# Two attention layers of a four-layer network on one core: the values' bias on VectorE, an earlier flag, and a first normed half block made one stage ahead

## The chip, the cores and the metric

The kernel runs on one core of a Trainium2 chip. The time is the device time of one execution in microseconds. A core has a matrix engine (TensorE, PE in the profile, with its weight loads as PEld), a vector engine (VectorE, DVE), an engine for activation functions (ScalarE, ACT), a general engine (GpSimd, POOL), and queues for transfers (SP is the one used here for weights and outputs). The engines run side by side, each in the order of its own program, and wait for one another by semaphores. Matrix products write to PSUM, a small memory of banks; everything else lies in SBUF, a memory of 128 partitions.

## The reference

The input x is 2 x 512 channels x 32 x 32 positions in float32, so every image is a matrix of 512 x 1024. Four layers follow one another, each on the output of the one before:

- Layer 0: attention on sampled positions with a learned position bias, and then an MLP of two products.
- Layer 1: linear attention with normalized queries and keys.
- Layers 2 and 3: plain attention. The two differ only in the number of groups of the normalization (8 and 32), and the change touches these two. Cut to what is computed:

```
xn   = group_norm(x) * w + b                    # per image
q,k,v = qkv_w @ xn + qkv_b                      # 512 x 1024 each, 8 heads of 64 channels
attn = softmax(q.T @ k * 64**-0.5, axis=keys)   # 1024 x 1024 for each head
out  = v @ attn.T                               # 64 x 1024 for each head
x    = x + proj_w @ out + proj_b
```

Because the weights of a softmax sum to 1, the bias of the values can be added to the result of a head instead of to the values. The kernel does so.

## The kernel before

**Layers and their stages.** `layer0`, `mlp0` and `layer1` end near 2555 us of the span. Layers 2 and 3 are two calls of `attention` (L954), each of two stages. `queries_keys_values` (L990) makes the queries, keys and values of both images; `heads_bounded` (L1205) makes the softmax, the result of the heads, the projection and the sum with x. The x tiles (4 per image, 128 channels x 1024 positions) stay in SBUF from the first layer to the last.

**Normalization.** Means and variances of an image's channels come from `channel_means` (L1168, on VectorE, after an early load of ScalarE's square root table). `group_means` (L1179) averages them over a group by two small TensorE products, and ends with the scale `sc`. `offsets_of_norm` (L1199) makes the offset `off` by two small VectorE instructions. Each is made for image 0 in the stage in front: layer 2's at the end of `layer1` (L907 to L928), layer 3's in the last projections of layer 2's heads (L1301 to L1307). The offsets and the normed tiles come at the beginning of `queries_keys_values`.

**Queries, keys and values.** Each product of 512 x 512 by 512 x 1024 is done by seven products of half size instead of eight (P1 to P7, the order is P1, P2, P3, P6, P7, P5, P4). They need the normed image as four half blocks of 256 channels x 512 positions, and three sums of them. `norm` (L1020) makes half blocks 0, 2, 3, 1 in this order, each by two instructions, c = 0 on VectorE (L1028) and c = 1 on ScalarE (L1026). P1 needs block 0 alone. For each image the products of queries and keys come first (PE, L1046), then those of the values (L1065), with adds on VectorE (L1084) that collect them. The order of the four compute engines in this stage is the order in which the code emits, by a manual schedule (L1089).

**The flag.** The softmax subtracts no maximum as long as the logits are bounded. `largest` (L1149) works out a bound from the squares of queries and keys; it runs after the first three value products of an image. After all value products of image 1, two VectorE instructions make `ok` and `oki` (L1139, L1141), and ScalarE has a small Exp that loads its table ahead (L1143). Every engine reads `oki` into a register, and branches: `heads_bounded` if the bound holds, `heads_general` otherwise (L972). With these inputs the bound holds.

**Heads.** A unit is one image, one pair of heads and one half of the query positions: 2 x 4 x 2 = 16 units, each of 8 steps n, one for each 128 keys. A step is a score product s (L1229, 8 matmuls), an exp from PSUM to an e tile on ScalarE (L1233), an addition of e to one of two running sums, and a value product o (L1258, 8 matmuls, which adds up over the unit in PSUM). The sums: `some` = e0 + e1 + e3 + e5 on POOL (L1238, L1240), `sum` = e2 + e4 + e6 + e7 + some on VectorE (L1243, L1245 twice, L1247). Values follow scores two steps behind. At the end of a unit ScalarE copies one half of o into the place of the queries (L1267) and VectorE adds the other (L1268). `divide` follows at step 4 of the next unit: a product d with ones gives the column sums (L1275), ScalarE copies one half (L1279), VectorE adds the other (L1280), takes the reciprocal (L1281), multiplies (L1283), and ScalarE adds the values' bias (L1284). TensorE's order is written out by hand (L1288 to L1311); that of the other engines is set by the tile scheduler from the dependences.

**Buffers.** The pool `ps_s` has 2 score tiles of two PSUM banks each (tag s), the pool `ps_o` one tile for o and one for d. There are 6 e tiles, one `some`, two `sum`. The pool `norm` lives from layer 1 to the end; the normed half blocks r0 to r6 are in a pool of `queries_keys_values`.

**Projection.** `project_block` (L593) makes 128 rows of the projection of one image by 8 products (L598) and adds bias and x on VectorE (L607). It runs for image 0, then image 1, four blocks each; in layer 3 the output leaves from here by SP. In layer 2 the means of image 0 for layer 3 are taken within: all four `channel_means` and the first product of `group_means` ahead of the second block of image 1, the second product ahead of the third.

**Before layer 1.** Its weights (`layer1_weights`, L776) are loaded by SP, 1.31 MB for the weights and 0.33 MB for a bias spread over all partitions, into a pool whose space layer 0 uses earlier. `lb` tiles of layer 0 (L409) are loaded on the same queue.

Of the kernel before, what the change touches and what calls it, by code (L numbers as in the profile page):

```python
# [11 lines left out]
F32 = mybir.dt.float32  # L12
AF = mybir.ActivationFunctionType
ALU = mybir.AluOpType
# [38 lines left out]
class Net:  # L53
# [730 lines left out]
    def layer1(self, w, bias):  # L784
# [3 lines left out]
        with ExitStack() as ctx:  # L788
# [108 lines left out]
            for b in range(B):  # L897
                for h in range(2):
# [30 lines left out]

# [24 lines left out]
    def attention(self, k: int, weights, out, meanwhile=lambda: None):  # L954
# [3 lines left out]
        with ExitStack() as ctx:  # L958
# [9 lines left out]
            small_logits, got = self.queries_keys_values(k, weights, ones, data, meanwhile)  # L968
            if k == 2:
                self.means_tiles(3, 0)  # L970

            with self.tc.If(small_logits > 0) as cmp:  # L972
                self.heads_bounded(k, ones, data, out)
            with cmp.Else():
                self.heads_general(k, data)
                with ExitStack() as ctx2:
                    proj = self.projection_weights(self.pool(ctx2, f"a{k}_w_p"), k)
                    ps = self.pool(ctx2, f"a{k}_ps_p", 2, psum=True)
                    for b in range(B):
                        for o in range(CT):  # L980
                            acc = ps.tile([P, 2, HF], F32, tag="ps", name=f"pbg{k}{b}{o}")
                            self.project_block(acc, data[b][0], proj, f"pb{k}", b, o, out)
                    if k == 2:
                        for t in range(CT):
                            self.channel_means(3, 0, t)
                        for _ in self.group_means(3, 0, ps.tile([P, 2, HF], F32, tag="ps", name="gm3g")):
                            pass
            return got

    def queries_keys_values(self, k, weights, ones, data, meanwhile):  # L990
# [8 lines left out]
        with ExitStack() as ctx:  # L999
# [20 lines left out]
            def norm(b, r, i, c, eng):  # L1020

                t = 2 * (i // 2) + c
                _, sc, off = self.means[b]
                x = self.xs[b][t][:, (i % 2) * HF : (i % 2 + 1) * HF]
                if eng is act:
                    act.activation(r[i][:, c, :], x, AF.Identity, scale=sc[:, t : t + 1], bias=off[:, t : t + 1])  # L1026
                else:
                    vec.tensor_scalar(r[i][:, c, :], x, sc[:, t : t + 1], off[:, t : t + 1], ALU.mult, ALU.add)  # L1028

            def square(i, t, h, cm):  # L1030

# [56 lines left out]
            engines = {getattr(mybir.EngineType, e) for e in ("PE", "Activation", "DVE", "Pool")}  # L1088
            with self.tc.manual_schedule(engines=engines):  # L1089
                dqk = small.tile([P, CT], F32, tag="dqk", name=f"dqk{k}")  # L1090
                self.offsets_of_norm(k, 0)
                xns = [tiles(0)]
                for i in (0, 2, 3, 1):
                    for c in range(2):
                        norm(0, xns[0], i, c, (vec, act)[c])
                vec.tensor_tensor(dqk, self.colr(f"qb{k}", CT), self.colr(f"kb{k}", CT), ALU.subtract)
                for b in range(B):
                    r = xns[b]
# [26 lines left out]
                    for n, which in enumerate(("P1", "P2", "P3", "P6", "P7", "P5", "P4")):  # L1125
# [4 lines left out]
                        if n == 2:  # L1130
                            while late:
                                late.pop(0)()
                            self.largest(k, b, ones, cm, small, ps_g, flag)
                        if b == 0 and which in ("P1", "P2", "P3", "P7"):
                            i = {"P1": 0, "P2": 2, "P3": 3, "P7": 1}[which]
                            for c in range(2):
                                norm(1, xns[1], i, c, act)
                ok = small.tile([1, B], F32, tag="ok", name=f"ok{k}")
                vec.tensor_scalar(ok, flag, 480.0**2, None, ALU.is_le)  # L1139
                oki = small.tile([1, 1], mybir.dt.int32, tag="oki", name=f"oki{k}")  # L1140
                vec.tensor_tensor(oki, ok[:, 0:1], ok[:, 1:2], ALU.mult)  # L1141
                early = small.tile([P, 1], F32, tag="early", name=f"early{k}")
                act.activation(early, self.cols[:, 0:1], AF.Exp, scale=0.0)  # L1143
# [55 lines left out]
    def offsets_of_norm(self, k, b):  # L1199
# [2 lines left out]
        self.nc.vector.tensor_tensor(off, gm, sc, ALU.mult)  # L1202
        self.nc.vector.tensor_tensor(off, self.colr(f"gn_b{k}", CT), off, ALU.subtract)

    def heads_bounded(self, k, ones, data, out):  # L1205


# [5 lines left out]
        with ExitStack() as ctx:  # L1213
# [56 lines left out]
            def divide(unit):  # L1270
# [10 lines left out]
                nc.vector.reciprocal(t, t)  # L1281
                res = data[b][0][p][:, h * HF : (h + 1) * HF]
                nc.vector.tensor_tensor(res, res, t, ALU.mult)  # L1283
                nc.scalar.activation(res, res, AF.Identity, bias=self.col(f"vb{k}", p))  # L1284

            units = [(b, p, h, {}) for b in range(B) for p in range(CT) for h in range(2)]
            steps = [(unit, n) for unit in units for n in range(NB)]
            with self.tc.manual_schedule(engines={mybir.EngineType.PE}):  # L1288
# [9 lines left out]
                        divide(steps[i - NB][0])  # L1298
                for b in range(B):
                    for o in range(CT):  # L1300
                        if b == 1 and o > 0 and k == 2:  # L1301
                            if o == 1:
                                for t in range(CT):
                                    self.channel_means(3, 0, t)
                                steps = self.group_means(3, 0, ps_o.tile([P, 2, HF], F32, tag="d", name="gm3"))
                            else:
                                next(steps, None)  # L1307
                        acc = ps_s.tile([P, 2, HF], F32, tag="s", name=f"pb{k}{b}{o}")
                        self.project_block(acc, data[b][0], proj, f"pb{k}", b, o, out)
                        if b == o == 0:  # L1310
                            divide(units[-1])  # L1311

    def heads_general(self, k, data):
        with ExitStack() as ctx:
# [214 lines left out]
```

## Time and profile before

| quantity | value |
|---|---|
| median of 3 runs | 3470.4 us (3470.14 to 3472.15) |
| profiled execution: time, span | 3472.31 us, 3470.5 us |
| mean granted clock of TensorE | 0.995 |
| busy: TensorE, VectorE, ScalarE, GpSimd | 3403.5, 2296.9, 2034.2, 2078.3 us |
| layer 2: first product of queries and keys | 2553.39 us |
| layer 2: first score | 2705.72 us |
| layer 3: first product of queries and keys | 3013.08 us |
| layer 3: first score | 3163.97 us |
| one unit of the heads in regular running | 15.25 us |

The profile is of one execution. A line of its timeline gives start, busy time, engine, line of the code, operation, the tile written and the tiles read, their shapes and the count of instructions gathered in the line; in brackets stands how long the engine had been idle, and whose work ended that. The view of waits adds such idle times by the line that waited and the line it waited for. TensorE's matmuls are pipelined and their ends are modelled, so distances between starts say more than ends. A wait of an engine that has time to spare costs nothing.

### The profile page before, as it was taken

The numbers are of one execution on the slowest core, as the hardware profiler recorded it, in microseconds if no ns is written. First come the engines' busy times: TensorE is split into PE (matmuls) and PEld (weight loads), VectorE is DVE, ScalarE is ACT, GpSimd is POOL, SyncE is SP. The second block draws the span as 40 slices with busy tenths as digits, with TensorE's granted clock in tenths as the row PEclk, the third lists the DMA queues.
The fourth block names the chain that finished last, engine by engine and source line by source line (L and its number), as shares of the span: only waits on it lengthen the run. The fifth ranks groups of instructions, "written<-read, shape, count | busy, mean of one in ns | idle before, by whom it ended". The sixth has DMA issues, their size and how long they took to land.

```text
span 3470.5 us, 60111 instructions
## 1 busy us (share of the span) xinstructions
PE 3403.5 (98%) x25280; PEld 1260.8 (36%) x25280; DVE 2296.9 (66%) x2507; ACT 2034.2 (59%) x2132; POOL 2078.3 (60%) x1584
## 2 busy tenths in 40 slices
PE   7999999999999999999999999999999999999999
PEld 2333333333333333333333334444646433454333
DVE  6877777778767567777766665565465566455664
ACT  5877877887887687887887762111111566113661
POOL 4778777777787577787788873442233444234441
PEclk9999999999999999999999999999989999999999
DMA  5878777887887577777788862110000000000001
GB/s 152 157 140 159 150 155 146 157 156 143 158 158 143 111 156 146 155 156 146 152 163 156 162 162 78 37 49 24 1 1 25 25 1 2 1 0 13 1 1 50
DMA packets 103246, 342.64 MB, mean 99 GB/s; under 512 B 12720, under 2 KB 14384, under 8 KB 100144
## 3 DMA queue, kind: packets, MB, share of 16 engines
q0 software_dynamic: 73296, 266.90, 40.7%
q1 hardware_dynamic: 28656, 69.68, 6.7%
q8 instruction: 202, 3.31, 0.4%
q10 hardware_dynamic: 1008, 2.06, 0.2%
q14 instruction: 84, 0.69, 0.1%
HBM read 67.27 MB, written 4.46 MB: 21 GB/s over the span
## 4 chain that ended last, share of the span: by engine, by line
PE 88%; DVE 7%; ACT 2%; POOL 1%; issue 1%; DMA 0%; ACTq 0%; DVEq 0%; SPq 0%; POOLq 0%
PE hp L486 45%; PE s L1229 6%; PE o L1258 6%; DVE h L455 3%; PE pb L598 3%; PE sim L518 3%; PE qk20P L1046 1%; PE qk30P L1046 1%; PE m_0P L649 1%; PE m_5P L649 1%; PE m_3P L649 1%; PE m_2P L649 1%; PE qk31P L1046 1%; PE qk21P L1046 1%; PE m_6P L649 1%; PE m_1P L649 1%
## 5 line engine op out<-in xcount | busy, mean ns | idle before, releaser
L486 PE MATMUL hp<-h,w 128*32 128x512 f32 x16384 | 1833.1, 594 | 5.5 <-DVE h L455 3.5
L455 DVE CUSTOM_DVE_ANT_1 h<-tx,bank 128x1024 f32<-128x1024 f32 x1024 | 1180.9, 1216 | 333.2 <-PE hp L486 310.2
L491 ACT ACTIVATE h<-hp,magb 128x1024 f32<-128x1024 f32 x1024 | 1122.3, 1111 | 418.9 <-PE hp L486 417.0
L486 PEld LDWEIGHTS hp<-h,w 128*32 128x32 f32 x16384 | 545.6, 110 | 1215.5 <-issue 1119.7
L478 POOL DMA_DIRECT2D h<-h x509 | 451.7, 1025 | 393.2 <-ACT h L497 334.2
L504 POOL TENSOR_TENSOR h<-h,h 128x1024 f32<-128x1024 f32 x255 | 613.6, 2406 | 21.3
L502 POOL TENSOR_SCALAR h<-h,flip 128x1024 f32<-128x1024 f32 x256 | 448.3, 1751 | 0.9 <-ACT h L491 0.9
L1233 ACT ACTIVATE e<-s 128x1024 f32<-128x1024 f32 x256 | 254.7, 1020 | 119.9 <-PE s L1229 119.9
L493 ACT ACTIVATE h<-h,flip 128x1024 f32<-128x1024 f32 x256 | 291.2, 1138 | 0.0
L1229 PE MATMUL s<-q,k 64*64 64x512 f32 x2048 | 263.1, 596 | 14.9 <-ACT e L1233 11.2
L1258 PE MATMUL o<-e,v 64*64 64x512 f32 x2048 | 261.4, 592 | 2.4 <-ACT e L1233 2.4
L1240 POOL TENSOR_TENSOR some<-some,e 128x1024 f32<-128x1024 f32 x64 | 151.2, 2362 | 85.8 <-ACT e L1233 83.4
L495 POOL TENSOR_SCALAR h<-h,flip 128x1024 f32<-128x1024 f32 x128 | 145.0, 1133 | 78.7 <-ACT h L491 77.3
L1238 POOL TENSOR_TENSOR some<-e,e 128x1024 f32<-128x1024 f32 x32 | 75.8, 2368 | 190.5 <-DVE sum L1247 152.5
L497 ACT ACTIVATE h<-h,flip 128x1024 f32<-128x1024 f32 x128 | 145.6, 1138 | 0.0
L518 PE MATMUL sim<-h,ends 128*32 128x512 f32 x1024 | 141.1, 592 | 0.0
L1229 PEld LDWEIGHTS s<-q,k 64*64 64x64 f32 x2048 | 75.3, 133 | 167.4 <-issue 104.9
L1243 DVE TENSOR_TENSOR sum<-e,e 128x1024 f32<-128x1024 f32 x32 | 39.4, 1232 | 139.8 <-ACT e L1233 139.8
L1258 PEld LDWEIGHTS o<-e,v 64*64 64x64 f32 x2048 | 75.2, 133 | 149.8 <-issue 123.7
L1034 POOL TENSOR_TENSOR sq<-q 128x512 f32<-128x512 f32 x32 | 33.2, 1039 | 144.2 <-DVE q L1053 100.1
L708 ACT ACTIVATE mh<-mh,cols 128x512 f32<-128x512 f32 x64 | 46.2, 722 | 124.2 <-DVE mh L726 65.5
L628 POOL TENSOR_TENSOR mlp_w<-mlp_w 128x512 f32<-128x512 f32 x16 | 22.4, 1400 | 161.1 <-DMA mlp_w<-in_mlp_w 125.5
(456 smaller groups left out, 3293.1 us busy)
## 6 DMA issues: line engine op xcount, KB each, us to landing
h<-h POOLq DMA_DIRECT2D x509, 512.0 KB, 6.5
lb<-logs SPq DMA_DIRECT2D x63, 512.0 KB, 5.2
mlp_w<-in_mlp_w SPq DMA_DIRECT2D x16, 1024.0 KB, 4.9
x<-in_x SPq DMA_DIRECT2D x8, 512.0 KB, 9.8
qkw<-in_l_qk SPq DMA_DIRECT2D x2, 2048.0 KB, 8.3
out<-x SPq DMA_DIRECT2D x16, 256.0 KB, 2.1
vw<-in_l_v SPq DMA_DIRECT2D x2, 1024.0 KB, 7.5
proj<-in_l_proj SPq DMA_DIRECT2D x8, 256.0 KB, 4.6
```

Source lines behind the costliest of these rows:

```text
L455: self.nc.vector._custom_dve(TENSOR_ADD_SAT, out=h[:, k, :, :], in0=x[:, jj, 2 * r + k, :].unsqueeze(1).to_broadcast([P, H, W]), in1=y[:, ...
L478: nc.gpsimd.dma_start(to, what, accum_op=ALU.add)
L486: nc.tensor.matmul(hp[rows, cut], lhsT=self.l0w2[:, 32 * q : 32 * q + 32], rhs=h1[k][:, cut], start=True, stop=True)
L491: nc.scalar.activation(y, hp, AF.Relu, bias=self.magb[:, q : q + 1])
L493: nc.scalar.activation(ys[0], ys[0], AF.Copy, scale=self.flip[:, 0:1])
L502: nc.gpsimd.tensor_scalar(y, y, self.flip[:, 2:3], 1.0, ALU.mult, ALU.mult)
L504: (nc.vector if final else nc.gpsimd).tensor_tensor(y, y, ys[2], ALU.add)
L518: nc.tensor.matmul(sims[u][at : at + 32, :], lhsT=self.ends[:, 28 - 4 * o : 60 - 4 * o], rhs=z[jj][:, h * HF : (h + 1) * HF], start=(o == ...
L649: self.nc.tensor.matmul(acc[p], lhsT=w[:, a, k, p * P : (p + 1) * P], rhs=right(r, k), start=k == 0, stop=k == 1)
L1229: nc.tensor.matmul(s[halves[c], par, :], lhsT=ks[p][rows, at : at + DH], rhs=qs[p][rows, cut], start=True, stop=True)
L1233: nc.scalar.activation(e, s, AF.Exp, scale=DH**-0.5)
L1258: nc.tensor.matmul(o[halves[par], r, :], lhsT=v[n // 2][rows, n % 2, at : at + DH], rhs=e[rows, par, :], start=(n == 0), stop=(n == NB - 1),)
```

## The change

It has five parts, all in layers 2 and 3.

1. The values' bias in `divide` is added by VectorE, in place, instead of by ScalarE.
2. `ok`, `oki` and the early Exp are emitted right after `largest` of image 1, that is after the first three of the seven value products instead of after all.
3. Half block 0 of the normed image has a tile of its own in the pool `norm` (4 KB more of each partition). `norm_first` makes the offsets and this half block for image 0: at the end of `layer1` for layer 2, and after the second product of `group_means`, behind the third projection block of image 1, for layer 3. The other blocks are made where they were.
4. The third score tile of the first unit takes the place of d in `ps_o`, and not one of the two score tiles.
5. `channel_means` of layer 3 is called one tile at a time after the projection blocks 1 to 4 of layer 2; the two products of `group_means` come at the same places of TensorE's order as before.

TensorE's and POOL's programs keep their orders. On VectorE 32 bias instructions come in, each between L1283 and the next L1245; on ScalarE 32 go. As the pool `norm` is larger, SP loads layer 1's weights and bias at another place: between two loads of `lb` late in layer 0 instead of after the MLP's first weights.

```diff
@@ layer1 @@
             self.means_tiles(2, 0)
+            self.first = {2: self.first_block(2, 0)}
...
                             if b == h == 1 and t % 2:
                                 next(steps, None)
+                self.norm_first(2)
@@ attention @@
             if k == 2:
                 self.means_tiles(3, 0)
+                self.first[3] = self.first_block(3, 0)
@@ queries_keys_values @@
             def tiles(b):
-                return [xpool.tile([P, 2, HF], F32, tag=f"r{i}", name=f"xn{k}{b}{i}") for i in range(7)]
+                first = self.first[k] if b == 0 else self.first_block(k, 1)
+                return [first] + [xpool.tile([P, 2, HF], F32, tag=f"r{i}", name=f"xn{k}{b}{i}") for i in range(1, 7)]
...
-                self.offsets_of_norm(k, 0)
                 xns = [tiles(0)]
-                for i in (0, 2, 3, 1):
+                for i in (2, 3, 1):
                     for c in range(2):
-                        norm(0, xns[0], i, c, (vec, act)[c])
+                        self.norm_block(k, 0, xns[0][i], i, c, (vec, act)[c])
...
                             self.largest(k, b, ones, cm, small, ps_g, flag)
+                            if b == B - 1:
+                                ok = small.tile([1, B], F32, tag="ok", name=f"ok{k}")
+                                vec.tensor_scalar(ok, flag, 480.0**2, None, ALU.is_le)
+                                oki = small.tile([1, 1], mybir.dt.int32, tag="oki", name=f"oki{k}")
+                                vec.tensor_tensor(oki, ok[:, 0:1], ok[:, 1:2], ALU.mult)
+                                early = small.tile([P, 1], F32, tag="early", name=f"early{k}")
+                                act.activation(early, self.cols[:, 0:1], AF.Exp, scale=0.0)
...
+    def first_block(self, k, b):
+        return self.norm.tile([P, 2, HF], F32, tag="first", bufs=1, name=f"xn{k}{b}0")
...
+    def norm_first(self, k):
+
+        self.offsets_of_norm(k, 0)
+        for c in range(2):
+            self.norm_block(k, 0, self.first[k], 0, c, (self.nc.vector, self.nc.scalar)[c])
@@ heads_bounded @@
-                s = ps_s.tile([P, 2, HF], F32, tag="s", name=f"s{k}{b}{p}{h}{n}")
+
+                third = unit is units[0] and n == 2
+                s = (ps_o if third else ps_s).tile([P, 2, HF], F32, tag="sd"[third], name=f"s{k}{b}{p}{h}{n}")
...
                 nc.vector.tensor_tensor(res, res, t, ALU.mult)
-                nc.scalar.activation(res, res, AF.Identity, bias=self.col(f"vb{k}", p))
+                nc.vector.tensor_scalar(res, res, self.col(f"vb{k}", p), None, ALU.add)
...
-                        if b == 1 and o > 0 and k == 2:
-                            if o == 1:
-                                for t in range(CT):
-                                    self.channel_means(3, 0, t)
-                                steps = self.group_means(3, 0, ps_o.tile([P, 2, HF], F32, tag="d", name="gm3"))
-                            else:
-                                next(steps, None)
...
+                        if k == 2:
+                            n = b * CT + o
+                            if 1 <= n <= CT:
+                                self.channel_means(3, 0, n - 1)
+                            elif n == CT + 1:
+                                steps = self.group_means(3, 0, ps_o.tile([P, 2, HF], F32, tag="d", name="gm3"))
+                                next(steps)
+                            elif n == CT + 2:
+                                next(steps, None)
+                                self.norm_first(3)
```

More of the change, by code (lines that the diff above doesn't have):

```diff
@@ L1017, in tiles @@
             def tiles(b):
-                return [xpool.tile([P, 2, HF], F32, tag=f"r{i}", name=f"xn{k}{b}{i}") for i in range(7)]
[L1020 to L1026, printed above, removed]
-                else:
-                    vec.tensor_scalar(r[i][:, c, :], x, sc[:, t : t + 1], off[:, t : t + 1], ALU.mult, ALU.add)
+                first = self.first[k] if b == 0 else self.first_block(k, 1)
+                return [first] + [xpool.tile([P, 2, HF], F32, tag=f"r{i}", name=f"xn{k}{b}{i}") for i in range(1, 7)]
             def square(i, t, h, cm):
@@ L1136, in queries_keys_values @@
                             for c in range(2):
[L1137 to L1143, printed above, removed]
+                                self.norm_block(k, 1, xns[1][i], i, c, act)
             with self.tc.manual_schedule(engines={mybir.EngineType.SP}):
@@ L1203, in offsets_of_norm, with norm_block @@
         self.nc.vector.tensor_tensor(off, self.colr(f"gn_b{k}", CT), off, ALU.subtract)
+    def first_block(self, k, b):
+        return self.norm.tile([P, 2, HF], F32, tag="first", bufs=1, name=f"xn{k}{b}0")
+    def norm_block(self, k, b, to, i, c, eng):
+        t = 2 * (i // 2) + c
+        _, sc, off = self.means[b]
+        sc, off = sc[:, t : t + 1], off[:, t : t + 1]
+        x = self.xs[b][t][:, (i % 2) * HF : (i % 2 + 1) * HF]
+        if eng is self.nc.scalar:
+            eng.activation(to[:, c, :], x, AF.Identity, scale=sc, bias=off)
+        else:
+            eng.tensor_scalar(to[:, c, :], x, sc, off, ALU.mult, ALU.add)
+    def norm_first(self, k):
+        self.offsets_of_norm(k, 0)
+        for c in range(2):
+            self.norm_block(k, 0, self.first[k], 0, c, (self.nc.vector, self.nc.scalar)[c])
     def heads_bounded(self, k, ones, data, out):
@@ L1300, in heads_bounded @@
                     for o in range(CT):
-                        if b == 1 and o > 0 and k == 2:
-                            if o == 1:
-                                for t in range(CT):
-                                    self.channel_means(3, 0, t)
-                                steps = self.group_means(3, 0, ps_o.tile([P, 2, HF], F32, tag="d", name="gm3"))
-                            else:
-                                next(steps, None)
                         acc = ps_s.tile([P, 2, HF], F32, tag="s", name=f"pb{k}{b}{o}")
@@ L1311, in heads_bounded @@
                             divide(units[-1])
+                        if k == 2:
[7 more added lines that the diff above has]
+                                next(steps, None)
+                                self.norm_first(3)
     def heads_general(self, k, data):
```

## The prediction

> **What bounds the kernel now.** I read the page's busy shares first, then the chain that ended last, then TensorE's waits after 2100 us, and then the timelines around each of those waits.
>
> ```profile
> PE 3403.5 (98%) x25280; PEld 1260.8 (36%) x25280; DVE 2296.9 (66%) x2507; ACT 2034.2 (59%) x2132; POOL 2078.3 (60%) x1584
> PE 88%; DVE 7%; ACT 2%; POOL 1%; issue 1%; DMA 0%; ACTq 0%; DVEq 0%; SPq 0%; POOLq 0%
> ```
>
> TensorE is busy 98% of the span and carries 88% of the chain. The change gives it the same instructions in the same order, so it can win only idle time of TensorE, or stretches at its lower clock. In layers 2 and 3 that idle time is short:
>
> ```profile
> PE s L1229 <- ACT e L1233: 11.2, 30, 0.8
> PE qk30P L1046 <- issue: 4.2, 1, 4.2
> PE s L1229 <- DVE oki L1141: 3.7, 2, 2.0
> PE qk20P L1046 <- DVE xn L1028: 2.9, 1, 2.9
> PE o L1258 <- ACT e L1233: 2.4, 2, 1.2
> ```
>
> (total, times, longest.) Together 24.4 us, and each line is touched by one part of the change. Ends of matmuls are modelled, so I take real gaps from starts: a unit's regular steps start every 0.858 us.
>
> [...]L1243 at 2851.59 began 0.36 us ahead of the end of POOL's L1240 (2849.58 + 2.37 = 2851.95) and took 1.44 us instead of 1.23, ending 1.08 us after POOL. So such an add may start about 0.15 us before POOL's end for nothing, and loses what is beyond. [...]Here one lasts 0.542 us (L1028) and the next starts 0.46 us later, less than an add of two tensors (0.69, 0.61). [...]after the 4.2 us gap loads come 0.85 us apart instead of 0.43, and the 1.97 us gap ahead of layer 2's heads was also followed by the lower clock, the 1.73 us gap of layer 3 not.
>
> **Part 1, bias from ScalarE to VectorE (32 times).** One unit of the heads (8 steps) lasts 15.25 us, where TensorE's 17 groups would take 17 x 0.858 = 14.58. The unit's boundary:
>
> ```profile
> 2750.93 0.72 ACT L1284 ACTIVATE q<-q,cols 128x512 f32<-128x512 f32 x1 [1.80 <-DVE q L1283]
> 2751.56 1.92 ACT L1233 ACTIVATE e<-s 128x1024 f32<-128x1024 f32 x2
> 2752.61 1.09 PE L1229 MATMUL s<-q,k 64*64 64x512 f32 x8 [0.34 <-ACT e L1233]
> 2752.59 1.23 DVE L1245 TENSOR_TENSOR sum<-sum,e 128x1024 f32<-128x1024 f32 x1 [0.56 <-ACT e L1233]
> 2755.39 0.69 DVE L1268 TENSOR_TENSOR q<-o,q 128x512 f32<-128x512 f32 x1 [0.24 <-ACT q L1267]
> 2757.74 2.36 POOL L1240 TENSOR_TENSOR some<-some,e 128x1024 f32<-128x1024 f32 x1
> ```
>
> ScalarE idles 1.80 us for L1283's product with its exps queued behind the bias; TensorE then waits for a score buffer. From starts (2751.23 + 0.858 = 2752.09 against 2752.61, and the next step) I take 0.57 us a unit. Without the bias, up to 2.5 us of slack opens on ScalarE, so this wait goes. But it does not follow that the unit shrinks by it, because two loops close at 15.25 us already.
> Loop A, the single o buffer: L1268's end (2740.83) frees o, two value steps and a score later comes e4 and L1243 at 2744.84 (4.01 us), then L1280, L1281 (3.35), L1283, two L1245, L1247, L1268, ending 2756.08 (11.24). In it are waits of 0.45 (second L1245) and some 0.3 (L1268) that go with ScalarE's delay; the bias puts in 0.57 (L1283 to L1245 is 0.61 start to start now, and becomes 0.72 for a dependent pair plus 0.46). New: 15.25 - 0.75 + 0.57 = 15.07.
> Loop B, POOL: L1247's end releases L1238, then L1240 (0.13 + 2.37 + 0.08 + 2.36 = 4.94), and L1243 of two SBUF inputs cannot run until that is over, less 0.15. From L1243 to L1247's end: 10.32 now, 10.32 - 0.45 + 0.57 = 10.44 after, less up to 0.08 if the adds follow one another more closely. New: 10.44 + 4.94 - 0.15 = 15.23, or 15.15.
> So the unit takes 15.15 to 15.23, and I take 15.19: 0.06 x 28 regular units (14 a layer) = 1.7 us gained. Bounds: bias at 0.46 and no dependence cost, 0.25 x 28 = 7 gained; a bias as dear as L1283 (0.72), 0.12 x 28 = 3.5 lost. At each layer's last unit no next unit follows: there the value step waited 1.20 (modelled; 1.39 by starts) for the exp behind the bias, and nothing takes its place: 2 x 1.39 = 2.8 gained.
>
> **Part 2, flag sooner and third score in another buffer.** These meet at the start of the heads:
>
> ```profile
> 2703.78 0.69 DVE L1084 TENSOR_TENSOR v<-vp21P,v 128x512 f32<-128x512 f32 x1 [1.03 <-PE vp21P L1065]
> 2704.57 0.15 DVE L1141 TENSOR_TENSOR oki<-ok 1x1 int32<-1x1 f32 x1
> 2705.72 3.49 PE L1229 MATMUL s<-q,k 64*64 64x512 f32 x16 [1.97 <-DVE oki L1141]
> 2707.66 1.28 ACT L1233 ACT_TABLE_LOAD   x1 [0.75 <-PE s L1229]
> 2710.03 2.00 PE L1229 MATMUL s<-q,k 64*64 64x512 f32 x16 [0.83 <-ACT e L1233]
> ```
>
> With the flag out by some 15 us earlier, its load and branch (oki to first score, 1.0 us) lie beside value products. What is left is the last v add (ends 2704.47), whose PSUM banks the scores take: first score at 2704.6 instead of 2705.72. The two new small VectorE instructions (0.15 each) fall in front of v adds that idle 1.03 us before each: nothing. The third score no longer waits for exp 0; the fourth takes the first's buffer after it. From score to exp 0: 1.31 at full clock (layer 3: 3163.97 to 3165.28) plus the table load's 1.30; then exp 1.08 and the fourth score 0.87. First value step: 2704.6 + 1.31 + 1.30 + 1.95 = 2709.15 against 2711.86: 2.7 us; 2.1 if the clock drops, which a gap of 0.9 makes unlikely. Layer 3 likewise, no table load: last v add ends 3162.97, score at 3163.1, value step at 3166.4 against 3168.18: 1.7 us.
>
> **Part 3, first normed half block in the stage in front.** Layer 3:
>
> ```profile
> 3001.77 7.11 PE L598 MATMUL pb<-q,proj 128*128 128x512 f32 x16
> 3008.92 1.41 DVE L607 SCALAR_TENSOR_TENSOR x<-pb,cols,x 128x512 f32<-128x512 f32 x2 [4.97 <-PE pb L598]
> 3011.97 0.11 DVE L961 MEMSET ones<- 128x64 f32 x1 [1.64 <-issue]
> 3013.08 15.67 PE L1046 MATMUL qk30P<-xn,qkw 128*128 128x512 f32 x32 [4.20 <-issue]
> ```
>
> TensorE has finished at 3008.88. Now VectorE adds (to 3010.33), branches (1.64), makes offsets and the block; after, offsets and block are made while the last projection runs (scale ready 3003.95, VectorE idle until 3008.92), four small steps and two of 0.54 and 0.8 in nearly 5 us: hidden. TensorE is then held by the last add alone, whose PSUM the products take, and starts at 10.33 + 0.15: 3010.48, 2.6 us earlier. The gap becomes 1.6 us, so I expect full clock: 32 products in 13.73 instead of 15.67, 1.9 more. VectorE's own branch still ends near 3012, and its next blocks are due only after P1's products. Layer 2's block is last in the same order (TensorE waits 2.9 us for xn, the offsets coming when the means do, 2552.65): 0.
>
> **At no cost.** The channel means spread over the projections leave VectorE's order and TensorE's as they are. The extra 4 KB of the norm pool shifts layer 1's weight load (L779, 1.31 MB and 0.33 MB for the bias) from 2077.5 to between two loads of lb in layer 0, about 1720. Landing 5.8 us against 30 us between lb loads: hidden. Even one delayed lb would cost at most some 6 us once; I enter it below nothing only as a chance.
>
> **Sum**: 1.7 + 2.8 + 2.7 + 1.7 + 2.6 + 1.9 = 13.4 us off the profiled span of 3470.5; the unprofiled median is 3470.4, so 3457.
>
> **Rivals.** (1) Heads fully TensorE-bound: neither loop holds, 16 us from 28 x 0.57, others 11.7: 3443. For it: waits vanish; against: both loops measured at 15.25. 8%. (2) New waits take the place of the old ones: the clock stays low at both starts (1.9 and 0.6 less) and the unit does not shrink (1.7 less): 9.2 us, 3461; if the unit grows by its bound of 0.12 us, 5.7 us, 3465. For it: loop B closes within 0.02 us of today's unit, and the gap of 1.6 us is near the 1.97 that brought the lower clock. 22%. (3) Slower: the bias slows the unit. It follows L1283 by nothing and POOL's third add ends only 1 us before it (2749.85 against 2750.9)[...]. The one-off gains are 11.7, so it breaks even at 11.7 / 28 = 0.42 us a unit, and ends 0.2% slower at 0.66; at 0.75 it gives 3480. Against it: a tensor_scalar's 0.46, and the waits of 0.75 in loop A that can absorb it. 4%. (4) The flag or the block does not do what it says, since TensorE's own branch still takes a microsecond after its last work: 4.4 us less without the one, 4.5 without the other, so 3461.5, or 3466 without both. For it: oki to first score is 1.0 us now; against: while the last projection ran, TensorE's sequencer had nothing else to do. 6%. The forecast itself, 3452 to 3461: 60%.
>
> **How the numbers follow.** 0.2% is 6.9 us, about what a measurement here can tell from none. Range 3448 to 3465: the forecast with the bounds of the unit (+3.5, -7) and the edges; outside lie (1), (3), a part of (4). Faster: all of the forecast and of (1), most of (2): 0.86. Same: the rest of (2) and (4): 0.10. Slower: 0.04.
>
> **What would show it.** TensorE's waits on oki gone, on exp in the heads almost so, and the wait for L1268 longer; unit period 15.15 to 15.23; bias row on VectorE 32 x about 0.54; qk30P's gap 1.6 and its row 13.7; layer 2's first value step some 5.4 us after the start of the last v add, where it is 8.1 now (2703.78 to 2711.86). The prediction is wrong if the period falls under 15.0 or rises over 15.4, or if the first scores still start a microsecond after the last v add's end.

## The result and the profile after

The changed kernel takes 3453.45 us (median of 4 runs, 3451.91 to 3454.01) against 3470.27 us for the kernel before in the same comparison (3466.68 to 3472.15). The ratio is 0.9952 with a 95% interval of 0.9935 to 0.9969: 16.8 us less, where 13.4 were forecast (3457, range 3448 to 3465). The profiled execution of the changed kernel has a span of 3450.1 us.

First the lines of its page on busy time and on the chain that ended last:

```profile
PE 3394.9 (98%) x25280; PEld 1260.6 (37%) x25280; DVE 2313.2 (67%) x2539; ACT 2017.4 (58%) x2100; POOL 2078.3 (60%) x1584
PE 80%; DVE 15%; ACT 2%; POOL 1%; issue 1%; DMA 0%; DVEq 0%; ACTq 0%; SPq 0%; POOLq 0%
```

32 instructions went from ScalarE to VectorE, and VectorE's share of the chain went from 7% to 15%. That is more than VectorE's added work of 16 us in a span of 3450: in the heads the chain now runs through VectorE. The view of TensorE's waits from 2000 us on (line and what it waited for: total, times, longest) names the place:

```profile
PE o L1275 <- DVE q L1285: 6.7, 28, 0.6
PE qk20P L1041 <- DVE xn L1212: 2.9, 1, 2.9
PE s L1246 <- DVE v L1079: 1.8, 2, 0.9
PE qk30P L1041 <- issue: 1.5, 1, 1.5
PE s L1246 <- ACT e L1250: 0.8, 1, 0.8
```

The 30 waits for an exp (11.2 us) have shrunk to one of 0.8, those for `oki` (3.7) to two of 0.9 for the last v add, and that of layer 3's first product from 4.2 to 1.5; the two of the last value steps (2.4) are gone. In their place stand 28 waits of the first value product of a unit for L1285, the add that frees the o tile. (Lines from L905 on have moved by a few numbers: L1229, L1233, L1243, L1245, L1247, L1258 and L1268 of before are L1246, L1250, L1260, L1262, L1264, L1275 and L1285.) VectorE at one boundary of units, and TensorE behind it, from the timeline of the changed kernel:

```profile
2745.82 0.49 DVE L1301 TENSOR_SCALAR q<-q,cols 128x512 f32<-128x512 f32 x1
2746.22 2.55 DVE L1262 TENSOR_TENSOR sum<-sum,e 128x1024 f32<-128x1024 f32 x2
2748.87 1.23 DVE L1264 TENSOR_TENSOR sum<-sum,some 128x1024 f32<-128x1024 f32 x1
2750.01 0.68 DVE L1285 TENSOR_TENSOR q<-o,q 128x512 f32<-128x512 f32 x1
2750.75 1.95 PE L1275 MATMUL o<-e,v 64*64 64x512 f32 x16 [0.22 <-DVE q L1285]
2754.68 1.45 DVE L1260 TENSOR_TENSOR sum<-e,e 128x1024 f32<-128x1024 f32 x1 [3.98 <-ACT e L1250]
```

VectorE works without a gap over 0.1 us up to L1285, and TensorE starts the unit as that ends. The unit before started the same line at 2735.70, so a unit takes 15.05 us.

To place the gain I cut both spans at starts that both have:

| from, to | before | after | difference |
|---|---|---|---|
| start of the span, layer 2's first product | 2553.39 | 2551.15 | -2.24 |
| to layer 2's first score | 152.33 | 151.25 | -1.08 |
| to its first value step | 6.14 | 4.55 | -1.59 |
| to its first projection (heads) | 240.16 | 235.79 | -4.37 |
| to layer 3's first product | 61.06 | 58.41 | -2.65 |
| to layer 3's first score | 150.89 | 148.34 | -2.55 |
| to its first value step | 4.21 | 3.45 | -0.76 |
| to its first projection (heads) | 240.05 | 236.15 | -3.90 |
| to the end of the span | 62.27 | 61.01 | -1.26 |

The first row and the last are not the change's. The first differs between profiles of kernels that share everything up to there (2551.2 here, 2551.9 to 2553.7 in the kernels below with the same front, and not by the place of layer 1's load). The last is the landing of the last output: from the first projection to the end of the last add the two kernels take 57.87 and 57.86 us. The other rows sum to 16.9 us, which is what the medians show (16.8).

### The profile page after: what moved, and what is told of

Same layout as the page of the kernel before. It is cut to its first block, busy times and chain, and to the rows that moved or that the text cites. A ratio compares the mean times of both kernels' runs of the same rounds, so it can differ in the third digit from the quotient of the medians.

```text
span 3450.1 us, 60119 instructions
## 1 busy us (share of the span) xinstructions
PE 3394.9 (98%) x25280; PEld 1260.6 (37%) x25280; DVE 2313.2 (67%) x2539; ACT 2017.4 (58%) x2100; POOL 2078.3 (60%) x1584
## 4 chain that ended last, share of the span: by engine, by line
PE 80%; DVE 15%; ACT 2%; POOL 1%; issue 1%; DMA 0%; DVEq 0%; ACTq 0%; SPq 0%; POOLq 0%
PE hp L486 46%; DVE h L455 3%; PE pb L598 3%; DVE r L1298 3%; PE sim L518 3%; PE o L1275 2%; DVE sum L1262 2%; PE s L1246 2%; PE qk20P L1041 1%; PE qk30P L1041 1%; PE m_0P L649 1%; PE qk21P L1041 1%; PE m_5P L649 1%; PE m_4P L649 1%; PE m_2P L649 1%; PE qk31P L1041 1%
## 5 line engine op out<-in xcount | busy, mean ns | idle before, releaser
L1250 ACT ACTIVATE e<-s 128x1024 f32<-128x1024 f32 x256 | 258.2, 1024 | 177.6 <-PE s L1246 164.1
L1275 PE MATMUL o<-e,v 64*64 64x512 f32 x2048 | 261.0, 592 | 6.7 <-DVE q L1285 6.7
L1246 PE MATMUL s<-q,k 64*64 64x512 f32 x2048 | 259.8, 589 | 2.6 <-DVE v L1079 1.8
L1260 DVE TENSOR_TENSOR sum<-e,e 128x1024 f32<-128x1024 f32 x32 | 46.4, 1451 | 136.1 <-ACT e L1250 136.1
L1275 PEld LDWEIGHTS o<-e,v 64*64 64x64 f32 x2048 | 75.8, 133 | 157.3 <-issue 123.7
L1246 PEld LDWEIGHTS s<-q,k 64*64 64x64 f32 x2048 | 78.7, 133 | 143.4 <-issue 117.9
```

What stands on the lines that cost most here:

```text
L1246: nc.tensor.matmul(s[halves[c], par, :], lhsT=ks[p][rows, at : at + DH], rhs=qs[p][rows, cut], start=True, stop=True)
L1250: nc.scalar.activation(e, s, AF.Exp, scale=DH**-0.5)
L1275: nc.tensor.matmul(o[halves[par], r, :], lhsT=v[n // 2][rows, n % 2, at : at + DH], rhs=e[rows, par, :], start=(n == 0), stop=(n == NB - 1),)
```

## The experiments

"Less" and "more" below are against the kernel before in the same comparison where a ratio is given, and otherwise by rows of the table above.

### The bias alone

```diff
-                nc.scalar.activation(res, res, AF.Identity, bias=self.col(f"vb{k}", p))
+                nc.vector.tensor_scalar(res, res, self.col(f"vb{k}", p), None, ALU.add)
```

> The kernel before with part 1 alone (bias on VectorE). Theory: the bias on ScalarE held the exps behind it at each unit's boundary, and what is left is the loop through the single o buffer; units go from 15.25 us to 15.05 and the two tails of 1.39 us go. From first value step to first projection 4.4 us less in layer 2 and 3.9 in layer 3, nothing elsewhere: about 8.3 us less than before, 3462. Rival (the bias costs VectorE what it saves ScalarE): units stay at 15.25, only the tails go, 2.8 us less, 3467.5.

Measured: 3461.19 us, ratio 0.9971 (0.9960 to 0.9982). Heads 4.32 us shorter in layer 2 and 4.27 in layer 3, the rows between them within 0.1 of before, units of 15.05 us. The theory's numbers hold, and the rival's 2.8 us is out.

### All but the bias

```diff
-                nc.vector.tensor_scalar(res, res, self.col(f"vb{k}", p), None, ALU.add)
+                nc.scalar.activation(res, res, AF.Identity, bias=self.col(f"vb{k}", p))
```

> The changed kernel with the bias back on ScalarE. Theory (the parts are independent): units at 15.25 and the tails back; starts of the heads and the front of layer 3 as in the changed kernel: 8.6 us less than before (1.1 + 1.6 + 2.65 + 3.3), about 3462. Rival (the gain of the edges rests on the shorter ScalarE queue): the first value steps come later than in the changed kernel, under 5 us less than before.

Measured: 3461.52 us, ratio 0.9974 (0.9963 to 0.9984). The heads are back at 240.16 and 240.09 us, the first value steps come 4.55 and 3.45 us after the first scores, as in the changed kernel. The parts do not need one another: this kernel's gain of 8.9 us and the bias's 9.3 sum to 18.2, which is the 16.8 of both within the intervals.

### The first half block alone

```diff
@@ the kernel before @@
+                self.norm_first(2)
...
+                                next(steps, None)
+                                self.norm_first(3)
```

> The kernel before with parts 3 and 5 alone (first normed half block made in the stage in front, means spread). Theory: the gap ahead of layer 3's first product falls from 4.2 to 1.55 us, TensorE keeps its clock and P1's 32 products take 13.7 instead of 15.67 us: 2.65 + 1.9 = 4.6 us less than before, 3466. Layer 2's front unchanged (gap 2.9). Rival: the products stay at the low clock without the other parts: 2.65 less. The other place of layer 1's weight load comes with this part: should layer 0 be shorter by 2 us here as in the changed kernel's profile, and not in the kernel with the bias alone, the load is its cause.

Measured: 3465.33 us, ratio 0.9986 (0.9979 to 0.9992). The first products of layer 3, from the timelines of the kernel with the bias alone, which has the old front (first line), and of this kernel (second):

```profile
3008.95 15.67 PE L1046 MATMUL qk30P<-xn,qkw 128*128 128x512 f32 x32 [4.21 <-issue]
3008.86 13.97 PE L1041 MATMUL qk30P<-xn,qkw 128*128 128x512 f32 x32 [1.55 <-issue]
```

The gap falls from 4.2 to 1.55 us, and the 32 matmuls (a product of float32 stands as two matmuls in the trace) take 1.70 us less, since TensorE kept its clock: the granted clock was 1.00 from 3008.8 us on, where the kernel before had 0.53 in its first 3 us. 2.65 + 1.70 = 4.35 of the expected 4.6. Layer 2's front is as before (2.93). At the start of the MLP this kernel stands at 2090.48, between the changed kernel (2089.18), the bias alone (2091.48) and all but the bias (2091.54, which has the other place of layer 1's load as well): the load does not shorten layer 0.

### The start of the heads: parts 2 and 4, and part 2 alone

```diff
@@ both @@
                             self.largest(k, b, ones, cm, small, ps_g, flag)
+                            if b == B - 1:
+                                ok = small.tile([1, B], F32, tag="ok", name=f"ok{k}")
...
@@ parts 2 and 4 only @@
+                third = unit is units[0] and n == 2
+                s = (ps_o if third else ps_s).tile([P, 2, HF], F32, tag="sd"[third], name=f"s{k}{b}{p}{h}{n}")
```

> The kernel before with parts 2 and 4 alone (flag sooner, third score in d's place). Theory: first score 0.9 us after the last value product instead of 1.97 and 1.73, and the third score waits for no exp: layer 2's first value step 2.7 us sooner, layer 3's 1.4 to 1.7: 4.2 us less than before, 3466. Rival (each engine still pays its branch after the last value product): under 1 us.

> The kernel before with part 2 alone (flag sooner; the third score stays in the score pool). Theory: the first score starts 0.9 us after the last value product in both layers (1.1 and 0.85 us sooner), and the third score waits for the first exp as before: first value steps 1.8 to 2.0 us sooner in layer 2 and 0.85 in layer 3, so 2.7 of the 4.2 us that parts 2 and 4 bring together. Rival (the exps set the first value step and the flag only moves the wait): first value steps unchanged.

Measured: parts 2 and 4 3467.11 us, ratio 0.9989 (0.9980 to 0.9997); part 2 alone 3468.23, ratio 0.9994 (0.9984 to 1.0003), which cannot be told from no change. The profiles are clearer. The start of layer 2's heads with part 2 alone, and in the changed kernel:

```profile
2703.88 1.95 PE L1230 MATMUL s<-q,k 64*64 64x512 f32 x16 [0.88 <-DVE v L1084]
2707.53 2.00 PE L1230 MATMUL s<-q,k 64*64 64x512 f32 x16 [1.70 <-ACT e L1234]
2709.35 1.90 PE L1259 MATMUL o<-e,v 64*64 64x512 f32 x16
...
2702.40 2.81 PE L1246 MATMUL s<-q,k 64*64 64x512 f32 x24 [0.88 <-DVE v L1079]
2706.04 1.09 PE L1246 MATMUL s<-q,k 64*64 64x512 f32 x8 [0.84 <-ACT e L1250]
2706.95 1.90 PE L1275 MATMUL o<-e,v 64*64 64x512 f32 x16
```

In both the first score waits 0.88 for the last v add and no longer for `oki` (1.97). With part 2 alone the third score waits 1.70 for an exp, and the first value step comes 5.47 us after the first score; with part 4 three scores run on, and it is 4.55 (6.14 before). So part 4 is worth 0.9 of layer 2's 2.7 us, and 0.75 in layer 3.

The flag moves the first score by 1.1 us. What is left of the 2.7, 0.67 (6.14 less 5.47), is clock: behind the gap of 1.97 us TensorE's granted clock was 0.59 in the kernel before (its first 16 score matmuls took 3.49 us, where they took 1.95 with part 2 alone), and 0.57 behind 1.98 in the kernel with the bias alone, but 1.00 behind the same gap of 1.98 in the kernel with the half block alone, which has the old flag and takes 5.47 too. So those 0.67 us are not lost in every execution.

Both kernels also show what makes the small terms of layer 3 hard to time: its first 32 matmuls, behind gaps of 4.06 and 4.15 us, took 16.38 and 16.55 us here, and 15.67 behind 4.20 before. That is a difference of up to 0.9 us between profiles, as much as the flag gains there.

### Where the unit's 15.05 us come from: no bias

```diff
-                nc.vector.tensor_scalar(res, res, self.col(f"vb{k}", p), None, ALU.add)
```

> The changed kernel without the values' bias at all (leaves L1301 out). Theory (loop A, from o's release to o's release through VectorE, sets the unit): 0.53 to 0.57 us leave that loop, which would close at 14.5, under TensorE's 14.58; units near 14.6 to 14.65 and TensorE's waits for L1285 gone: 28 x 0.43 = 12 us less than the changed kernel, 3441. Rival (loop B, POOL's two adds and the hold of L1260, sets it): the hold takes back what the bias frees only where POOL is last, units 14.7 to 14.85, 6 to 10 us less.

Measured: 3442.48 us, ratio 0.9918 (0.9898 to 0.9938). The kernel leaves the bias out, so its result lacks it, and only its time is of use. Units of 14.65 to 14.68 us (one of 14.84), no wait for L1285 left, heads of 230.63 and 230.47. The bias on VectorE thus costs 0.38 us a unit, 10.6 us in 28: it is in the loop that sets the unit. Which of the two loops that is does not follow from this run, because the bias lies in both: the stretch from L1260's start to L1264's end shrinks from 10.44 to 9.85 us for either. At most boundaries L1260 now starts 0.12 to 0.25 us before POOL's second add ends, and takes 1.22 to 1.33 us.

### More work for TensorE inside the loop

```diff
+                if n == 4:
+                    for c in range(2):
+                        at = n * P + c * DH
+                        nc.tensor.matmul(
+                            s[halves[c], 0, :], lhsT=ks[p][halves[0], at : at + DH], rhs=qs[p][halves[0], cut], start=True, stop=True
+                        )
```

> The changed kernel with two of the four score products of step 4 of every unit done twice (0.43 us more of TensorE's work in a unit, the result is the same). TensorE's own work becomes 15.01 us, still under the 15.05 of a unit. Theory (loop A: o's release, two value steps, the score of step 4, its exp, L1260, and so on to o's release): the 0.43 lies in that loop and the unit grows by all of it, to 15.48: 13 us more in the span. Rival (TensorE's idle 0.47 us a unit is free to use, POOL's loop sets the unit): units stay under 15.15, at most 3 us more.

Measured: 3478.4 us (one run), units of 15.85 us. Two lines of this kernel's timeline:

```profile
2736.98 0.68 DVE L1291 TENSOR_TENSOR q<-o,q 128x512 f32<-128x512 f32 x1
2742.47 1.23 DVE L1266 TENSOR_TENSOR sum<-e,e 128x1024 f32<-128x1024 f32 x1 [4.81 <-ACT e L1256]
```

The way from o's release to the first add of `sum` grew from 4.01 to 4.81 us, and the unit from 15.05 to 15.85: the same 0.80. I had priced the two products at 0.43, half of a step. By this growth the two, both on one half of the rows, took 0.80. So the size was expected wrongly, but the growth is one to one: loop A had no slack in the changed kernel, or part of the 0.80 would have gone into it. TensorE still waits 28 times for L1291 (5.6 us), so its idle time there is not free. POOL is done before L1266 begins, and L1266 is back at 1.23 us: here only the loop through o can set the unit.

### The bias on GpSimd

```diff
-                nc.vector.tensor_scalar(res, res, self.col(f"vb{k}", p), None, ALU.add)
+                nc.gpsimd.tensor_scalar(res, res, self.col(f"vb{k}", p), None, ALU.add)
```

> The changed kernel with the bias on GpSimd, which is idle for 5.5 us of each unit behind its third add. [...]GpSimd's tensor_scalar (about 0.6 to 0.8 us for 512 columns, half of L495's 1.13 for 1024) holds VectorE's L1262 with two SBUF inputs beside it, so VectorE gains nothing by the move: units 15.05 to 15.3, time the same as the changed kernel to 7 us more. Rival (no hold for a single-input instruction): units fall to 14.65, 11 us less than the changed kernel.

Measured: 3448.17 us, ratio 0.9934 (0.9918 to 0.9951), units of 14.85 us: between the 15.05 to 15.3 that were expected of a hold and the rival's 14.65.

```profile
2747.41 2.85 DVE L1262 TENSOR_TENSOR sum<-sum,e 128x1024 f32<-128x1024 f32 x2
2747.66 2.40 POOL L1301 TENSOR_SCALAR q<-q,cols 128x512 f32<-128x512 f32 x1 [1.31 <-DVE q L1300]
```

The two adds of VectorE beside it take 2.85 instead of 2.55 us, the first 1.22 as ever and the second 1.53. So VectorE pays 0.30, where a bias of its own put 0.52 into the loop (from L1300 to the next add 1.13 us start to start, 0.61 before). GpSimd pays more: 2.40 us, where the last bias of each layer, with no add of two SBUF tensors beside it, took 1.56 (0.6 to 0.8 were expected). (The profile's durations on GpSimd are rough.) GpSimd has the time to spare: it is busy 2156.5 of 3446.4 us.

### The bias folded into the projection's

```diff
+                for o in range(CT):
+                    for t in range(CT):
+                        nc.tensor.matmul(
+                            fold[:, 0, o : o + 1],
+                            lhsT=proj[t][:, o * P : (o + 1) * P],
+                            rhs=self.col(f"vb{k}", t),
...
+                nc.vector.tensor_tensor(pv, fold[:, 0, 0:CT], self.colr(f"pb{k}", CT), ALU.add)
```

> The changed kernel with the bias folded into the projection's: 16 products of one column with the projection's weights, and one add, once a layer, give proj_w @ vb + proj_b, and the 32 bias instructions go. Theory: units as in the kernel without the bias (14.6 to 14.65), the small products cost 1.5 to 4 us a layer on TensorE (16 weight loads and short products at 0.1 to 0.2): 12 less 3 to 8, so 4 to 9 us less than the changed kernel, 3444 to 3449. Rival: the small products' wait for a score buffer at the end of the heads eats the gain: the same as the changed kernel.

Measured: 3452.6 us, ratio 0.9945 (0.9928 to 0.9961), the same as the changed kernel. Units are 14.65 to 14.68 us, and all of it is given back at the end of the heads:

```profile
2939.27 3.73 PE L1319 MATMUL fold<-cols,proj 128*128 128x1 f32 x32
2942.87 8.81 PE L598 MATMUL pb<-q,proj 128*128 128x512 f32 x16
3385.27 4.68 PE L1319 MATMUL fold<-cols,proj 128*128 128x1 f32 x32
3389.82 9.51 PE L598 MATMUL pb<-q,proj 128*128 128x512 f32 x16
```

The small products cost 3.6 and 4.55 us, start to start. The projection block behind them takes 8.81 and 9.51 us instead of 7.13 (a row of 16 matmuls elsewhere), since TensorE ran it in part at a lower clock: 0.64 was granted from 2943 to 2947 us. Not a buffer's wait, as the rival had it, but the same end. The profile is of the longest of four executions (3450.14, 3450.35, 3454.85 and 3455.13 us), so the clock may have cost less in the two short ones; no profile of them shows it.

### The bias on ScalarE, later in its queue

```diff
-            with self.tc.manual_schedule(engines={mybir.EngineType.PE}):
+            with self.tc.manual_schedule(engines={mybir.EngineType.PE, mybir.EngineType.Activation}):
...
                     if i % NB == 4 and NB < i < len(steps):
                         divide(steps[i - NB][0])
+                    if i % NB == 3 and i > 2 * NB:
+                        bias(steps[i - 2 * NB][0])
```

`bias` is the old ScalarE instruction, taken out of `divide`.

> The changed kernel with the bias back on ScalarE, but at another place: ScalarE's order in the heads is written out as TensorE's is, with a unit's bias nine exps further on, after the exp of step 3 of the next unit, where ScalarE idles 1.5 us (0.72 needed). Theory: what cost time in the kernel before was not the 0.72 us of the instruction but its place at the head of ScalarE's queue, 1.80 us before its input was there, with the exps behind it; here neither ScalarE nor VectorE's loop pays: units as without the bias, 14.65 to 14.7, 10.9 us less than the changed kernel, about 3443. Rival (a bias on ScalarE takes its own time from the exps wherever it stands): units 14.9 to 15.25, the same as the changed kernel or slower.

Measured: 3441.38 us, ratio 0.9914 (0.9897 to 0.9931): 29.4 us less than before, and faster than the changed kernel. Units of 14.65 to 14.68 us, as without any bias. ScalarE's timeline:

```profile
2749.69 1.94 ACT L1250 ACTIVATE e<-s 128x1024 f32<-128x1024 f32 x2 [0.22 <-PE s L1246]
2751.51 0.72 ACT L1305 ACTIVATE q<-q,cols 128x512 f32<-128x512 f32 x1
2753.13 1.02 ACT L1250 ACTIVATE e<-s 128x1024 f32<-128x1024 f32 x1 [0.89 <-PE s L1246]
```

The same 0.72 us as before, now between two exps with 0.89 us of idle time left behind it, and nothing waits. As ScalarE's order is written out here, more than the bias could have moved. But the traces show its instructions in the heads in the same order as in the changed kernel, but for the biases and one thing at the start of layer 2. There the scheduler of all the other kernels puts the load of the square root table (L1167), which is needed only in the projections, ahead of the heads. It undoes the early Exp of part 2, and exp 0 loads its table again (1.28 us). Here that load comes behind the exps; layer 2's first value step is 3.46 us after the first score instead of 4.55, and 0.3 of this is lost again in the first unit. So some 0.8 of the 29.4 us is not the bias's, and other parts of it are the flag's and the half block's. The kernel to compare with is all but the bias, which differs from this one in the bias's place and in that load alone: its heads take 240.16 and 240.09 us, and these 230.93 and 230.44. This settles what the bias cost there and in the kernel before: its place in the queue, not its duration.

## Why the prediction was right, and where it was off

- **The units.** Forecast 15.15 to 15.23 us, measured 15.05 (but for one of 15.40 at the change of image in layer 3); 1.7 us forecast for 28 units, 5.6 measured (28 x 0.20). This is the term that was mis-sized, and it more than makes up the 3.5 us between 13.4 and 16.9; the others came out within 0.2 of their forecasts. The step that failed is the end of loop B: "such an add may start about 0.15 us before POOL's end for nothing, and loses what is beyond". The changed kernel at one boundary, engine by engine:

```profile
2737.62 2.36 POOL L1257 TENSOR_TENSOR some<-some,e 128x1024 f32<-128x1024 f32 x1
2739.66 1.41 DVE L1260 TENSOR_TENSOR sum<-e,e 128x1024 f32<-128x1024 f32 x1 [4.01 <-ACT e L1250]
2740.29 0.59 ACT L1296 COPY r<-d 128x512 f32<-128x512 f32 x1 [0.67 <-PE d L1292]
2740.99 0.68 DVE L1297 TENSOR_TENSOR r<-d,r 128x512 f32<-128x512 f32 x1
```

For the add itself the sentence held. L1260 starts 0.33 us before POOL's end, as soon as its exp is there, and takes 1.41 us instead of 1.23: 0.18 late, which is 0.33 less 0.15. But the unit does not lose that. The next step, L1297, needs ScalarE's copy of d (L1296) too, and that ends 1.22 us after L1260's start in any case. Unheld, the step starts 0.03 us after the copy, 1.25 after the start of the add (so L1280 in the kernel before, and L1297 in the kernel without the bias); held, it starts 1.33 after it, 0.08 before the add ends. Of the 0.18 us only 0.08 reach the chain. In all twelve profiles the step starts 0.03 us after the copy or 0.08 before the end of the add, whichever is later, at each of 360 boundaries to within 0.01 us. The prediction had put the whole delay into the unit, and so 15.23.

So loop A set the unit: 15.07 forecast, 15.05 measured. That the two are so close is in part luck: the 15.07 has no term for the 0.08 us of the hold, but the bias put in 0.52 instead of 0.57, and 0.80 us of waits and small steps went instead of 0.75. In the same way L1260's start to L1264's end is 10.44 us as worked out, with the hold in it. That loop A is the bound was shown by the added products; leaving the bias out shows only that VectorE's stretch, which both loops share, lies in it. What POOL's adds would do to the unit if they started sooner was not measured: with a second tile for `some`, the pool that it was put into would need 16 KB of each partition, where 14.66 are left.

- **The bias on VectorE.** L1301, with one tensor of 512 columns as input, takes 0.486 us; L1300, which multiplies two tensors of that size in SBUF, takes 0.691. L1300 to L1262 is 1.13 us start to start (1.18 forecast).
- **The tails.** 2 x 1.39 forecast. In the changed kernel TensorE runs from the last score through three value steps into the projection (2940.05, 24 matmuls, then 2942.74) with no wait; heads minus units leave 4.3 - 14 x 0.20 = 1.5 a layer in the kernel with the bias alone.
- **Flag and third score.** First score 0.84 us after the start of layer 2's last v add (0.82 forecast), first value step 5.39 after it (5.4 forecast). Layer 3: score 0.85 sooner and value step another 0.75: 1.6 of 1.7. Of layer 2's 2.7 us, 0.67 is the low clock of the profile before, which another execution behind the same gap did not have.
- **The half block.** Gap 1.55 (1.6 forecast), 32 matmuls in 13.97 us (13.7 forecast), so 2.65 + 1.70 of 2.6 + 1.9. The bet on the clock held in all eight profiles with this part (gaps of 1.55 to 1.70). Layer 2's front stayed at 2.93.
- **At no cost.** Layer 1's weights are issued at 1717.7, between `lb` loads at 1699.9 and 1731.8; their landing took 9.9 us instead of 5.8, still inside the gap. From the MLP to layer 1 and from there to layer 2 nothing moved (385.72 us in both, and 76.28 against 76.26).
- **The rivals.** Heads bound by TensorE alone (3443) was not this change, but it is what the later bias reaches, at 3441.38: the 28 x 0.57 us were there to be had, by another edit. Rivals 2 to 4 did not come: the clock held at both starts (1.00 granted behind gaps of 0.88 and 1.55 us), the unit shrank, and the flag and the block did what they say.

## What to carry to other kernels

When an instruction delays an engine that has time to spare, look at what stands behind it in that engine's queue and when its input arrives, before giving the work to another engine: the same instruction nine exps later cost nothing here, and on VectorE it cost 0.38 us of each unit. A wait that is removed is worth at most the distance to the next loop that closes; work out each loop, through buffers as well as through engines, and take the longest. A delay in a loop counts only as far as the next step was not waiting for something else: 0.18 us of hold came out as 0.08. And small products on the busiest engine can cost more than their own time, through the clock behind them (0.64 granted for 4 us in layer 2): 1.7 and 2.4 us here, beside 3.6 and 4.55.

## What the runs showed of the hardware

- Between GpSimd and VectorE's adds of two SBUF tensors: a VectorE add of 128 x 1024 (1.23 us alone) that began up to 0.15 us before the end of a GpSimd add lost nothing (1.22 to 1.23 us), and one that began more than 0.17 us before it ended 1.08 to 1.09 us behind GpSimd's end in all 143 cases (1.41 us long for an overlap of 0.33, 2.07 for 0.99). A GpSimd tensor_scalar of 128 x 512 that began 0.25 us after the first of two such adds took 2.40 us instead of 1.56; the first add kept its 1.22 us and the second took 1.53.
- TensorE's granted clock was 1.00 behind gaps of 1.55 us (layer 3's first product in the changed kernel) and 1.73 us (layer 3's first score in the kernel before), and 0.50 to 0.53 in the first 3 us behind gaps of 2.93, 2.94 and 4.20 us in these two kernels. The first 32 matmuls of a layer's queries and keys took 13.97 us behind gaps of 1.55 to 1.70 us (six profiles), and 15.40 to 16.88 us behind gaps of 2.93 to 3.12 and 4.06 to 4.21 us. Behind the same gap of 2.93 or 2.94 us layer 2's took 15.40 us in one profile and 16.88 in another. Behind gaps of 1.97 to 1.98 us the clock was lower in two of three profiles (0.59 and 0.57; 1.00 in the third). Behind the 16 products of a single column (32 matmuls, 3.6 and 4.55 us without a pause) 16 matmuls took 8.81 and 9.51 us, 7.13 elsewhere, with 0.64 granted from 2943 to 2947 us.
